# The second attention's result turned by VectorE squares and a way through memory

## The chip, the cores and the metric

The kernel runs on one core of one Trainium2 chip. The metric is the device time of one execution in microseconds, the median of three runs. The engines are TensorE (matrix products and its own transposes), VectorE, ScalarE, GpSimd and SyncE (SP). SP only issues transfers here; they run on the core's 16 DMA engines.

## The reference

Two layers act on x, 8 images of 128 channels and 48 x 48 = 2304 positions, all in fp32. This is what is computed, cut to what matters:

```
# layer 0: causal attention over the 2304 positions, added to x
q, k, v = lrelu(W{q,k,v} @ [group_norm(x), position rows] + b)
x = x + (softmax(mask(q^T k / sqrt(128))) * mask) @ v
# layer 1, on tokens t (2304 x 128 per image)
t = x as tokens
n = layer_norm(t)
t = t + softmax(n n^T) n                  # full attention, no weights
u = layer_norm(t) @ W^T                   # then batch norm over all tokens
y_i = sigmoid(u_i + y_{i-1} @ V^T)        # a recurrence along the tokens
return t + y
```

## The kernel before

**Chunks and batches.** An image is a batch b. Its 2304 positions are six chunks j of 384 tokens (NQ = 6, QC = 384), a chunk is three blocks of 128 (QB = 3). For each batch the class Causal does the first attention and the class Full the second, and a stream of items (one item is one block of keys or values against one chunk of queries) runs through all batches without a break. The first three items of the next batch's causal attention lie between the last items of the full one, and the projections of the next batch run in the full attention's chunks 4 and 5. After the last batch comes the recurrence in three groups.

**The order of the instructions.** It is written out by hand. Stream keeps a modelled time, now, and lists of pending steps (Chain), each with a cost and a due time. Each pass of the main loop emits the score product of item n, then the value product of item n - 3 (LAG), and then up to two due steps. Every engine works through its own instructions in just that order, and each transfer of SP waits at the head of SP's queue until what it needs is there.

**The full attention.** The score matrix is symmetric, so a square of it is used twice. For chunk j and a later chunk n the direct item makes scores (L1168), exponentials on ScalarE (L1170) and the product with the values (L1182). VectorE then transposes the square in 32 x 32 blocks (L1131), three of these make a tile, SP stores the tile as e(j,n) (L1111), and four loads bring it back transposed as g(j,n) (L1102). Chunk n then takes its products for the keys of chunk j from g (L1178). "Pair (1,5)" below is g(1,5): the squares of keys of chunk 1, used by chunk 5. There are three buffers for g, so a load can be issued when the third product with the tile three places before is done. Chunks 4 and 5 take four and five such tiles.

**The end of a chunk.** Full.after closes chunk j. ScalarE copies the result from PSUM (L1193). A chain of steps follows: the row sums (sums, with a small product on TensorE, L1205), then residual, in which TensorE transposes the result's three blocks (transposed, L931, the rows of_t), VectorE scales them, adds them to the tokens (L1224), takes the moments and makes a 32 x 32 transpose for the way to memory (L1231). Then come the roots on GpSimd (rooted), a small transpose of them on VectorE (turn_root, L1242), the stores of roots and turned rows (spread, three transfers at L1248 and four at L1251), their loads in another layout (fetch, L1255 and L1257), a product with the weights (L1264), a scaling and statistics on VectorE (L1265, L1266) and a copy on ScalarE (stored, L1270). Once in a batch, after chunk 1, the rows kept for the output are stored (L1288, L1289). The last two chunks of the last batch take a shorter way without memory.

**Buffers.** chunk_tile hands out the chunk's tiles by tag. It remembers the holder of each buffer and the number of steps that the holder's chain must have done, and emits these first when they are still pending. The product results have two PSUM banks (ps_o), the scores four (ps_s), other small results two (ps_t).

Of the kernel before, what the change touches and what calls it, by code (L numbers as in the profile page):

```python
# [14 lines left out]
F32 = mybir.dt.float32  # L15
AF = mybir.ActivationFunctionType
ALU = mybir.AluOpType
# [587 lines left out]
def fast_path(ctx: ExitStack, tc: tile.TileContext, x, pe, w_ffn, out, x_tok, w_qkv, w_pos, v_t, gamma_beta, flag):  # L605
    nc = tc.nc
    B, C, H, W = x.shape
    N = H * W
    P = 128
# [52 lines left out]
    with ExitStack() as actx:  # L662
# [107 lines left out]
        for r in roots:  # L770
            nc.gpsimd.memset(r, 0.0)

        st = Stream()
        order = ExitStack()
        order.enter_context(tc.manual_schedule())
# [5 lines left out]
        def group_norm(b):  # L781
            xt = xbuf[b]
            c = {}

            def part1():
                gs = small2.tile([P, NQ, 6], F32, tag="gn_st", name=f"gn_st_{b}")
                for j in range(NQ):
                    nc.vector.bn_stats(gs[:, j, :], xt[:, ts(j, QC)])
                mv = small.tile([P, 2], F32, tag="gn_mv", name=f"gn_mv_{b}")
                nc.vector.bn_aggr(mv, gs)  # L790
                c["mv"] = mv

            def part2():
                mv = c["mv"]
                tp = psum_t(f"gn_m_{b}")
                nc.tensor.matmul(tp[:, 0:1], grp, mv[:, 0:1], start=True, stop=True)
                mg = small.tile([P, 1], F32, tag="gn_mg", name=f"gn_mg_{b}")
                nc.vector.tensor_copy(mg, tp[:, 0:1])
                d = small.tile([P, 1], F32, tag="gn_d", name=f"gn_d_{b}")
                nc.vector.tensor_sub(d, mv[:, 0:1], mg)  # L800
                e = small.tile([P, 1], F32, tag="gn_e", name=f"gn_e_{b}")
                nc.vector.scalar_tensor_tensor(e, d, d, mv[:, 1:2], ALU.mult, ALU.add)
                c["mg"], c["e"] = mg, e

            def part3():
                tp = psum_t(f"gn_v_{b}")
                nc.tensor.matmul(tp[:, 0:1], grp, c["e"], start=True, stop=True)
                rs = small.tile([P, 1], F32, tag="gn_rs", name=f"gn_rs_{b}")
                rsqrt(small, rs, tp[:, 0:1], 1e-5, "gn")
                norm_of[b] = c["mg"], rs  # L810

            return [(part1, 0.0, [("DVE", 3.6)]), (part2, 0.15, [("DVE", 0.6)]), (part3, 0.15, [("DVE", 0.15), ("POOL", 0.9)])]


# [85 lines left out]

        def bounds(b):

            qk = small.tile([P, 2], F32, tag="qk", name=f"qk_{b}")
            nc.vector.tensor_reduce(qk, largest[b], AX.X, ALU.max)
            nc.vector.tensor_mul(bound[:, b : b + 1], qk[:, 0:1], qk[:, 1:2])

# [27 lines left out]
        def turned_back(src, name):  # L934

            tp = psum_t(name)
            out_ap = tp[:, :QC].rearrange("p (a g r) -> p g a r", a=R, g=QB)
            for g in range(QB):
                nc.tensor.transpose(out_ap[:, g], src[:, ts(g, P)], ident)
            return tp  # L940

        def by_block(tile_ap):

            return tile_ap.rearrange("p (g a r) -> p a g r", a=R, g=QB)
# [6 lines left out]
        class Causal:  # L951
# [37 lines left out]
            def product(self, j, m, o, p, ready, first, last):  # L989
                b, off = self.b, self.offset(j, m)  # L990
                nc.tensor.matmul(o[:, off:QC], vals[b][:, ts(m, P)], p[:, off:], start=first, stop=last)  # L991
                st.spend((QC - off) * US, ready)

                if first:
                    self.sums[j] = (p, None)
                    return
                if self.sums[j][1] is None:
                    self.whose[j] = {}
                    a = chunk_tile("acc", f"acc_{b}_{j}", self.whose[j], 1)
                    if off:  # L1000
                        nc.vector.tensor_copy(a[:, :off], self.sums[j][0][:, :off])
                    nc.vector.tensor_add(a[:, off:], self.sums[j][0][:, off:], p[:, off:])
                    self.sums[j] = (None, a)
                else:
                    a = self.sums[j][1]
                    nc.vector.tensor_add(a[:, off:], a[:, off:], p[:, off:])  # L1006
                st.then(ready, [("DVE", 0.15 + (QC - off) * 0.00105)])

            def after(self, j, o):
# [1 line left out]
                cols = ts(j, QC)  # L1011
                acc = self.sums.pop(j)[1]
                c = self.whose.pop(j)
                o_sb = chunk_tile("o", f"oc_{b}_{j}", c, 3)
                nc.scalar.copy(by_block(o_sb), o[:, :QC].rearrange("p (a g r) -> p a g r", a=R, g=QB))
                at = st.then(st.now, [("ACT", 0.5)])

                y = t1p.tile([P, QC], F32, tag="t1t", name=f"t1t_{b}_{j}")
                nc.sync.dma_start(y, x_tok[b, j])
# [17 lines left out]
                    c["ri"] = ri  # L1037

                def residual():
                    to = transposed(o_sb, f"oc_t_{b}_{j}")  # L1040
                    for g in range(QB):
                        nc.vector.scalar_tensor_tensor(
                            y[:, ts(g, P)], to[:, ts(g, P)], c["ri"][:, g : g + 1], y[:, ts(g, P)], ALU.mult, ALU.add
                        )
                    t1_tok[b, j] = y
                    c["mv"], c["ve"] = moments(y, f"c{b}_{j}", "l1")
# [12 lines left out]
                def back():  # L1059
                    tp = transposed(c["y"], f"tb_{b}_{j}")  # L1060
                    nc.scalar.copy(x_hat[b][1][:, cols], tp[:, :QC])

                c["chain"] = normed_chunks[b, j] = st.add([
                    (turn, 0.0, [("DVE", 1.05)]),
                    (sums, 0.15, [("DVE", 0.55)]),
                    (residual, 0.35, [("DVE", 2.6)]),
                    (rooted, 0.0, [("POOL", 0.9)]),
                    (normed, 0.0, [("DVE", 1.1)]),
                    (back, 0.35, [("ACT", 0.5)]),
# [2 lines left out]
        class Full:  # L1072
# [115 lines left out]
            def after(self, j, o):  # L1188
                b, rows, tsum = self.b, self.rows, self.tsum
                cols = ts(j, QC)  # L1190
                c = {}
                o_sb = chunk_tile("o", f"of_{b}_{j}", c, 2)
                nc.scalar.copy(o_sb, o[:, :QC])  # L1193
                at = st.then(st.now, [("ACT", 0.5)])
                last = b == B - 1 and j >= NQ - 2

                def sums():

                    dn = small.tile([P, QB], F32, tag="dn", name=f"dn_{b}_{j}")
                    nc.vector.tensor_reduce(dn, rows[:, QB * j : QB * (j + 1), : j + 1], AX.X, ALU.add)  # L1200
                    n = NQ - 1 - j
                    if n:
                        tp = psum_t(f"ts_{b}_{j}")
                        k = n * R * QB
                        nc.tensor.matmul(  # L1205
                            tp[:, :k], same.rearrange("p a c -> p (a c)"), tsum[j][:, :n, :].rearrange("p n k -> p (n k)"),
                            start=True, stop=True,
                        )
                        own = small2.tile([P, NQ - 1, R, QB], F32, tag="own", name=f"own_{b}_{j}")
                        nc.vector.tensor_mul(  # L1210
                            own[:, :n].rearrange("p n a g -> p (n a g)"), tp[:, :k], mine[:, :n].rearrange("p n a g -> p (n a g)")
                        )
                        more = small.tile([P, QB], F32, tag="more", name=f"more_{b}_{j}")
                        nc.vector.tensor_reduce(more, own[:, :n].rearrange("p n a g -> p g (n a)"), AX.X, ALU.add)
                        nc.vector.tensor_add(dn, dn, more)
                    ri = small.tile([P, QB], F32, tag="ri", name=f"ri_{b}_{j}")
                    nc.vector.reciprocal(ri, dn)
                    c["ri"] = ri

                def residual():  # L1220
                    tp = transposed(o_sb, f"of_t_{b}_{j}")
                    t2 = chunk_tile("t2", f"t2_{b}_{j}", c, 5 if last else 2, bufs=1)
                    for g in range(QB):
                        nc.vector.scalar_tensor_tensor(  # L1224
                            t2[:, ts(g, P)], tp[:, ts(g, P)], c["ri"][:, g : g + 1], t1_tok[b, j][:, ts(g, P)], ALU.mult, ALU.add
                        )
                    c["t2"] = t2
                    c["mv"], c["ve"] = moments(t2, f"f{b}_{j}", "l2")
                    if not last:
                        c["tt"] = chunk_tile("turn", f"tt_{b}_{j}", c, 5, bufs=1)  # L1230
                        nc.vector.transpose(  # L1231
                            c["tt"].rearrange("p (k g r) -> p g k r", k=R, g=QB), t2.rearrange("p (g k c) -> p g k c", g=QB, k=R)
                        )
# [17 lines left out]
                        nc.sync.dma_start(d[r], c["tt"][ts(r, SQ)].rearrange("c (k f) -> c k f", k=R))  # L1251

                def fetch():
                    c["t2x"] = chunk_tile("t2x", f"t2x_{b}_{j}", c, 7, bufs=1)
                    nc.sync.dma_start(c["t2x"], t2_d[:, b, cols])  # L1255
                    c["scale"] = chunk_tile("scale", f"scale_{b}_{j}", c, 8, bufs=1)
                    nc.sync.dma_start(c["scale"], c["rs_d"][0].partition_broadcast(P))  # L1257

                def product():
# [56 lines left out]
                else:  # L1316
# [5 lines left out]
                        (stored, 0.0, [("ACT", 0.85)]),  # L1322
                    ]
                c["chain"] = self.before["chain"] = st.add([
                    (sums, 0.15, [("DVE", 0.8)]),
                    (residual, 0.35, [("DVE", 3.2)]),
                    (rooted, 0.0, [("POOL", 0.9)]),
                    *steps,
                ], max(at, st.free["DVE"]) + 0.2 - st.now)
# [236 lines left out]
```

## Time and profile before

| | |
|---|---|
| median of three runs | 1795.67 us (1794.95 to 1795.85) |
| the profiled execution | 1795.9 us |
| its span | 1793.8 us |
| TensorE busy | 1757.0 us, 98% |
| VectorE, ScalarE, GpSimd busy | 1298.0, 751.6 and 217.0 us |
| bytes moved | 240.35 MB, 134 GB/s in the mean |
| TensorE's transposes of the second attention's result (L931, of_t) | 144, in 48 groups of three |
| VectorE's transposes of squares (L1131) | 360 of 128x384, 550 ns each |
| ScalarE's copies of the result (L1193) | 48, 479 ns each |
| turned rows to memory (L1251) | 184 transfers of 48 KB |

The span is from the first to the last instruction of the profiled execution. Busy times are sums over the span; those of TensorE are modelled, since products are pipelined. Times in the timelines count from the start of the span. The granted clock of TensorE was 0.991 in the mean.

### The profile page before, as it was taken

The page shows a single profiled execution, that of the slowest core. Times are in us where ns is not written, and L with a number is a line of the kernel's source. Part 1 is how long each engine was busy: PE and PEld are TensorE (multiplying, and loading weights), DVE is VectorE, ACT ScalarE, POOL GpSimd, SP SyncE. Part 2 cuts the span into 40 slices and gives each one's busy share as a digit, 9 for nine tenths or more (in the row PEclk, how much of TensorE's full clock was granted, in tenths as well). Part 3 has the DMA queues.
Part 4 walks back from the last instruction along what each step waited for, and adds up shares of the span by engine and source line. Part 5 has one row for each costly group of instructions (what it writes and reads, how often), then busy time and mean ns, then how long its engine had stood idle before and what let it go on. Part 6 is the DMA issues. An engine that isn't in the chain of part 4 may idle for free.

```text
span 1793.8 us, 22009 instructions
## 1 busy us (share of the span) xinstructions
PE 1757.0 (98%) x6363; PEld 1106.4 (62%) x6363; DVE 1298.0 (72%) x3321; ACT 751.6 (42%) x1852; POOL 217.0 (12%) x305
## 2 busy tenths in 40 slices
PE   8999999999999999999999999999999999999995
PEld 5666566665666566665666656665666656665574
DVE  5768668766887668686687668876686866876477
ACT  2344434443345424444344433454234443444354
POOL 1100011000210002000110002100020001100016
PEclk8999999999999999999999999999999999999998
DMA  4205662257314583056622573145830566025857
GB/s 151 102 1 190 180 166 82 74 181 192 109 62 132 162 217 106 1 188 179 167 83 74 182 187 113 63 132 163 216 106 1 183 183 172 27 72 182 201 179 200
DMA packets 176774, 240.35 MB, mean 134 GB/s; under 512 B 66209, under 2 KB 146242, under 8 KB 176644
## 3 DMA queue, kind: packets, MB, share of 16 engines
q1 hardware_dynamic: 175692, 235.83, 44.7%
q0 software_dynamic: 720, 2.62, 1.0%
q8 instruction: 53, 0.87, 0.2%
q14 instruction: 77, 0.63, 0.1%
q10 hardware_dynamic: 232, 0.40, 0.1%
HBM read 142.37 MB, written 96.41 MB: 133 GB/s over the span
## 4 chain that ended last, share of the span: by engine, by line
PE 95%; DVE 2%; DMA 1%; SPq 1%; issue 1%; ACT 0%; POOL 0%; DVEq 0%; ACTq 0%; POOLq 0%
PE s L1168 18%; PE o L1182 18%; PE s L980 17%; PE o L991 16%; PE o L1178 12%; PE pj L871 4%; PE pj L874 2%; PE z L1483 2%; PE wx L1264 2%; PE oc_t L931 1%; PE tb L931 1%; PE of_t L931 1%; SPq L1102 1%; DVE r L1465 0%; PE pb L829 0%
## 5 line engine op out<-in xcount | busy, mean ns | idle before, releaser
L1170 ACT ACTIVATE p<-s,shift 128x384 f32<-128x384 f32 x504 | 293.1, 582 | 491.3 <-PE s L1168 482.4
L982 ACT ACTIVATE p<-s 128x384 f32<-128x384 f32 (+2 forms) x504 | 233.0, 463 | 426.2 <-PE s L980 389.1
L1168 PE MATMUL s<-xh 128*128 128x384 f32 x1008 | 410.3, 489 | 0.0
L1182 PE MATMUL o<-p,xhT 128*128 128x384 f32 x1008 | 403.9, 487 | 4.4 <-ACT p L1170 4.4
L980 PE MATMUL s<-q,k 128*128 128x384 f32 (+2 forms) x1008 | 381.4, 460 | 0.1
L991 PE MATMUL o<-p,vT 128*128 128x384 f32 (+2 forms) x1008 | 378.3, 457 | 0.0
L1178 PE MATMUL o<-g,xhT 128*128 128x384 f32 x720 | 281.5, 488 | 1.4 <-DMA g<-e 1.3
L1182 PEld LDWEIGHTS o<-p,xhT 128*128 128x128 f32 x1008 | 189.0, 190 | 132.3 <-ACT p L1170 8.7
L991 PEld LDWEIGHTS o<-p,vT 128*128 128x128 f32 x1008 | 189.0, 191 | 114.7 <-issue 0.6
L1168 PEld LDWEIGHTS s<-xh 128*128 128x128 f32 x1008 | 186.1, 190 | 115.0
L1006 DVE TENSOR_TENSOR acc<-acc,p 128x384 f32<-128x384 f32 (+2 forms) x408 | 211.1, 517 | 48.9 <-ACT p L982 18.0
L980 PEld LDWEIGHTS s<-q,k 128*128 128x128 f32 x1008 | 180.9, 191 | 90.8 <-issue 0.9
L1131 DVE STREAM_TRANSPOSE t<-p 128x384 f32<-128x384 f32 x360 | 187.3, 550 | 37.6 <-ACT p L1170 36.2
L1178 PEld LDWEIGHTS o<-g,xhT 128*128 128x128 f32 x720 | 133.0, 190 | 84.1 <-issue 2.7
L1139 DVE TENSOR_REDUCE tsum<-t 128x12 f32<-128x1152 f32 x120 | 162.3, 1353 | 4.2
L876 DVE TENSOR_TENSOR z<-pj,pb 128x384 f32<-128x384 f32 x144 | 79.0, 548 | 105.2 <-PE pj L871 88.3
L985 POOL TENSOR_TENSOR p<-p,triu 128x128 f32<-128x128 f32 x144 | 83.4, 586 | 547.6 <-ACT p L982 417.2
L1237 POOL TENSOR_TENSOR roots<-ve_f,mhalf 128x3 f32<-128x3 f32 x48 | 40.8, 849 | 553.0 <-DVE ve_f L915 553.0
L1170 ACT ACTIVATION_READ_ACCUMULATOR p<-s,shift 128x1 f32 x504 | 98.0, 194 | 0.0
L871 PE MATMUL pj<-xn,wT 128*128 128x384 f32 x192 | 80.4, 504 | 1.4 <-DVE xn L864 1.4
L921 POOL TENSOR_TENSOR rs_c<-ve_c,mhalf 128x3 f32<-128x3 f32 x48 | 46.9, 977 | 245.7 <-DVE ve_c L915 245.7
L1224 DVE SCALAR_TENSOR_TENSOR t<-of_t,ri,t1t 128x128 f32<-128x128 f32 x144 | 41.5, 343 | 33.2 <-PE of_t L931 33.2
(262 smaller groups left out, 1492.2 us busy)
## 6 DMA issues: line engine op xcount, KB each, us to landing
e<-t SPq DMA_DIRECT2D x120, 576.0 KB
g<-e SPq DMA_DIRECT2D x480, 144.0 KB
pb<-posb_d SPq DMA_DIRECT2D x46, 576.0 KB
t1t<-in_x_tok_dram SPq DMA_DIRECT2D x48, 192.0 KB
t_d<-tt SPq DMA_DIRECT2D x184, 48.0 KB
t2x<-t_d SPq DMA_DIRECT2D x46, 192.0 KB
scale<-rs SPq DMA_DIRECT2D x46, 192.0 KB
x<-in_x_dram SPq DMA_DIRECT2D x14, 576.0 KB
```

What stands on the lines that cost most here:

```text
L871: nc.tensor.matmul(ps[:, :QC], wT[:, j, :], xn, start=True, stop=True)
L980: nc.tensor.matmul(s[:, off:QC], keys[b][:, ts(m, P)], queries[b, j][:, off:], start=True, stop=True)
L982: nc.scalar.activation(p[:, off:], s[:, off:QC], AF.Exp, scale=SCALE)
L985: nc.gpsimd.tensor_mul(p[:, off : off + P], p[:, off : off + P], triu)
L991: nc.tensor.matmul(o[:, off:QC], vals[b][:, ts(m, P)], p[:, off:], start=first, stop=last)
L1006: nc.vector.tensor_add(a[:, off:], a[:, off:], p[:, off:])
L1131: nc.vector.transpose(t[:, :, :, g, :].rearrange("p b j r -> p j b r"), p.rearrange("p (j b r) -> p j b r", j=QB, b=R))
L1139: nc.vector.tensor_reduce(self.tsum[j][:, n - j - 1, :], t.rearrange("p b j m r -> p (b j) (m r)"), AX.X, ALU.add)
L1168: nc.tensor.matmul(s[:, :QC], xh[:, ts(m, P)], xh[:, ts(j, QC)], start=True, stop=True)
L1170: nc.scalar.activation(p, s[:, :QC], AF.Exp, bias=shift, accum_out=self.rows[:, m, j : j + 1])
L1178: nc.tensor.matmul(out_ap, xhT[:, QB * i + g, :], p, start=first, stop=last)
L1182: nc.tensor.matmul(o[:, :QC], xhT[:, what[1], :], p, start=first, stop=last)
```

## The change

The result of a chunk of the full attention is no longer copied by ScalarE and transposed by TensorE. VectorE transposes it from PSUM in 32 x 32 blocks into an SBUF tile (turn_result). SP stores this tile to a tensor in memory, and four transfers load it back so that the blocks stand where a whole transpose would put them (token_major). These are two new steps ahead of sums, each with 5 us in the model. residual then reads the loaded tile (block_of) and emits no TensorE instruction. This is so for all chunks but the last three of the last batch, 45 of 48. The two flags are constants: CAUSAL_FAR is False, so the causal attention keeps its way, and FULL_FAR is True. Step counts given to chunk_tile rise by two where the chain is longer, and some small tiles move from a pool with three buffers to one with two.

```diff
+        def turn_result(o, name, holder, blocks_first):
+
+            ot = chunk_tile("o", f"ot_{name}", holder, 1)
+            dst, src = ot.rearrange("p (a g c) -> p a g c", a=R, g=QB), o[:, :QC]
+            if blocks_first:
+                dst, src = dst.rearrange("p a g c -> p g a c"), src.rearrange("p (g a r) -> p g a r", a=R, g=QB)
+            else:
+                src = src.rearrange("p (a g r) -> p a g r", a=R, g=QB)
+            nc.vector.transpose(dst, src)
+            return ot
+
+        def token_major(holder, ot, name, tag, steps):
+
+            d = dpool.tile([P, QC], F32, tag=f"o_{tag}", name=f"o_d_{name}")
+
+            def store():
+                nc.sync.dma_start(d, ot)
+
+            def load():
+                holder["o"] = to = chunk_tile(tag, f"to_{name}", holder, steps, bufs=1)
+                src = d.rearrange("(k r) (a f) -> a r k f", r=SQ, a=R)
+                for r in range(R):
+                    nc.sync.dma_start(to[ts(r, SQ)].rearrange("r (k f) -> r k f", k=R), src[r])
+
+            return [(store, 0.0, [("", 5.0)]), (load, 0.0, [("", 5.0)])]
+
+        def block_of(to, g):
+
+            return to.rearrange("p (k g c) -> p g k c", g=QB, c=SQ)[:, g]
...
-                o_sb = chunk_tile("o", f"of_{b}_{j}", c, 2)
-                nc.scalar.copy(o_sb, o[:, :QC])
-                at = st.then(st.now, [("ACT", 0.5)])
                 last = b == B - 1 and j >= NQ - 2
+                far = FULL_FAR and not (b == B - 1 and j >= NQ - 3)
+                if far:
+                    ot = turn_result(o, f"f_{b}_{j}", c, True)
+                    at = st.then(st.now, [("DVE", 0.57)])
+                    through = token_major(c, ot, f"f_{b}_{j}", "tof", 4)
+                else:
+                    o_sb = chunk_tile("o", f"of_{b}_{j}", c, 2)
+                    nc.scalar.copy(o_sb, o[:, :QC])
+                    at = st.then(st.now, [("ACT", 0.5)])
+                    through = []
+                F = len(through)
...
                 def residual():
-                    tp = transposed(o_sb, f"of_t_{b}_{j}")
-                    t2 = chunk_tile("t2", f"t2_{b}_{j}", c, 5 if last else 2, bufs=1)
+                    tp = None if far else transposed(o_sb, f"of_t_{b}_{j}")
+                    t2 = chunk_tile("t2", f"t2_{b}_{j}", c, 5 if last else 2 + F, bufs=1)
                     for g in range(QB):
+                        aps = t2[:, ts(g, P)], t1_tok[b, j][:, ts(g, P)]
+                        if far:
+                            aps = [i.rearrange("p (k c) -> p k c", k=R) for i in aps]
                         nc.vector.scalar_tensor_tensor(
-                            t2[:, ts(g, P)], tp[:, ts(g, P)], c["ri"][:, g : g + 1], t1_tok[b, j][:, ts(g, P)], ALU.mult, ALU.add
+                            aps[0], block_of(c["o"], g) if far else tp[:, ts(g, P)], c["ri"][:, g : g + 1], aps[1], ALU.mult, ALU.add
                         )
...
                 c["chain"] = self.before["chain"] = st.add([
+                    *through,
                     (sums, 0.15, [("DVE", 0.8)]),
-                    (residual, 0.35, [("DVE", 3.2)]),
+                    (residual, 0.0 if far else 0.35, [("DVE", 3.2)]),
                     (rooted, 0.0, [("POOL", 0.9)]),
                     *steps,
                 ], max(at, st.free["DVE"]) + 0.2 - st.now)
```

## The prediction

> **What bounds the kernel now.** I read the page's busy shares and slices, then the chain that ended last, then the groups, then TensorE and the SP queue in order of time.
>
> ```profile
> PE 1757.0 (98%) x6363; PEld 1106.4 (62%) x6363; DVE 1298.0 (72%) x3321; ACT 751.6 (42%) x1852; POOL 217.0 (12%) x305
> DMA  4205662257314583056622573145830566025857
> ...
> PE 95%; DVE 2%; DMA 1%; SPq 1%; issue 1%; ACT 0%; POOL 0%; DVEq 0%; ACTq 0%; POOLq 0%
> ```
>
> TensorE sets the end: 98% busy and 95% of the chain. A microsecond taken out of its queue is a microsecond off the span, and a new stall of TensorE is one on it. The transfers are busy only in waves, one for each batch.
>
> The removed triples, in the timeline of TensorE:
>
> ```profile
> 161.83 0.81 PE L1178 MATMUL o<-g,xhT 128*128 128x384 f32 x2
> 162.47 0.49 PE L931 MATMUL of_t<-ident,of 128*128 128x128 f32 x3
> 162.80 0.81 PE L1168 MATMUL s<-xh 128*128 128x384 f32 x2
> ```
>
> The start of the triple and the start of the next product lie 0.33 us apart (327 to 328 ns in 46 of the 48 triples). That is its price in the queue, not the 0.49 us of modelled busy time. A full product takes 0.645 us from start to start (162.80 to 163.45).
>
> Next, what already makes TensorE wait: few things, and two matter here.
>
> ```profile
> PE o L1182 <- ACT p L1170: 4.4, 7, 0.6
> PE o L1178 <- DMA g<-e: 1.3, 1, 1.3
> ```
>
> Last, the transfers of the stored squares where they are densest, chunks 4 and 5 of the second attention, in SP's timeline of batch 0:
>
> ```profile
> 211.91 0.41 SPq L1288 DMA_DIRECT2D out_dram<-t2c  x1
> 212.37 2.73 SPq L1289 DMA_DIRECT2D t2l_d<-t2c  x1
> 215.20 2.22 SPq L1102 DMA_DIRECT2D g<-e  x4
> ...
> 218.46 1.80 SPq L1102 DMA_DIRECT2D g<-e  x4
> 220.36 0.38 SPq L842 DMA_DIRECT2D pb<-posb_d  x1
> 220.83 0.38 SPq L1111 DMA_DIRECT2D e<-t  x1
> 221.91 6.72 SPq L1102 DMA_DIRECT2D g<-e  x8
> 229.46 1.56 SPq L1248 DMA_DIRECT2D rs<-roots_t  x3
> 231.06 1.87 SPq L1251 DMA_DIRECT2D t_d<-tt  x4
> ```
>
> The busy time by window over the same stretch (columns: TensorE, weight loads, VectorE, ScalarE, GpSimd, granted clock, DMA share, GB/s):
>
> ```profile
> 220.00:232.00 12.00, 12.00 (x45) 7.45 (x44) 8.13 (x23) 3.57 (x9) 0.85 (x1) 1.00 1.02 263
> ```
>
> SP is issuing almost without a pause and the transfer engines are full (1.02). The reader is to see that the second resource near its limit is SP's queue with the transfers behind it, in these 35 us of every batch. Taking the trace's packets in the order of the issues, the load for pair (1,5) can be issued when its buffer is free, at 226.1; it is issued from 226.3 to 228.7, lands at 232.1 and is used at 234.5. The one load that TensorE did wait for landed 1.3 us before the product started, so 1.3 us of each such distance is no reserve: about 1 us is left.
>
> [...] The trace has VectorE's 128x384 transpose at 550 to 577 ns against 0.33 us of TensorE. [...] in the built order the first load of each chunk does wait for its store. [...] the packets here put the landing of loads 1.7 to 4.5 us after their last issue, so I use those.
>
> **The change, part by part.**
>
> Removed from TensorE: 45 triples (48 chunks less the last three) x 0.327 = 14.7 us, all on the chain.
>
> Removed from ScalarE: 45 copies x 0.479 = 21.6 us; ScalarE is 42% busy and this is off the path.
>
> Added to VectorE: 45 transposes from PSUM. There is no row for that source; the rows from SBUF say 0.55 to 0.58, and I take 0.57, 25.7 us (bounds: ScalarE's copy of the same tile from PSUM, 0.479, and three VectorE pieces of it from PSUM, 3 x 0.343 = 1.03). VectorE has the room: 72% busy, and it loses its 33.2 us of waits for of_t. The result's PSUM bank is freed by VectorE and no longer by ScalarE, but it is next written two chunks later, over 5 us, so a late VectorE costs nothing there. If that cover were gone, 0.5 us a chunk.
>
> A stall that goes. Once in each of the first seven batches VectorE stands before a residual, and what is behind it is late:
>
> ```profile
> 196.36 0.87 DVE L1224 SCALAR_TENSOR_TENSOR t<-of_t,ri,t1t 128x128 f32<-128x128 f32 x3 [1.04 <-PE of_t L931]
> 199.70 1.14 ACT L1270 COPY wx<-scale 128x384 f32<-128x384 f32 x1 [2.62 <-DVE scale L1265]
> 200.03 0.81 PE L1178 MATMUL o<-g,xhT 128*128 128x384 f32 x2
> 201.47 0.91 PE L1182 MATMUL o<-p,xhT 128*128 128x384 f32 x2 [0.63 <-ACT p L1170]
> ```
>
> ScalarE waits for the scaled product behind the residual, exponentials queue behind ScalarE's copy, and TensorE starts 0.8 us late, and its next product 0.1 more. In the new order that product stands before the residual with little ahead of it on VectorE, so I expect 7 x 0.9 = 6.3 us back (at worst 0).
>
> Added to SP's queue: a store and four loads for each chunk, about 0.38 + 4 x 0.43 = 2.1 us, 95 us in all. SP has pauses for that except in chunks 4 and 5. There the chain of each chunk is later by two steps, so the order changes too. From the third product on pair (0,4), which frees a buffer, SP now issues in this order up to the load of pair (1,5): roots 1.56, turned rows 1.87, g(3,4) 1.80, the new store of chunk 3 0.38, the kept rows 0.41 + 2.73, g(0,5) 1.80, positions 0.38, the four new loads of chunk 3 1.75, e(4,5) 0.38, g(1,5) 1.80; with 0.6 us between them, 15.5 us. The first must wait for VectorE's small transpose of the roots, which stands behind a projection's two operations (0.56 each): 1.0 us. So the last issue is at 16.5. In full-queue conditions it lands 4.3 us later (bounds 2.2 and 5.5; positions and e, 1.2 MB, are ahead of it), plus 1.3: ready at 22.1 (bounds 20.0 and 23.3). TensorE, counted along the new order, has 27 full products x 0.645, two narrow ones x 0.42 and one sum x 0.29 = 18.55 us from the same point to its first product with pair (1,5). It would stall 3.6 us (bounds 1.5 and 4.8). In the kernel before, the kept rows and the roots of chunk 2 lay ahead of g(2,4) and g(3,4), whose buffers are free 10.3 and 11.3 us before use; here the distance is 9.1. After this stall the queue is caught up: for (2,5) I get 1 to 2 us to spare. Seven batches: 25.2 us, nothing if the transfers keep up.
>
> The last batch has no projections on TensorE to hide it, but only chunks 0 to 2 change. The kept rows move between (3,4) and (0,5), ahead of the roots of chunk 3; the same sum gives a stall of 3.9 where it now has 1.2: +2.7.
>
> Other added waits: the residual on VectorE waits for its rows. Behind it stand projections' additions, which free score banks. In the order the rows are issued 9 or more products (5.8 us) ahead of it, so 0; if they come late, VectorE stands still and TensorE has about two free banks, 1.3 us, before it follows. The smaller pools hold values of one batch or of VectorE alone: 0.
>
> Sum: -14.7 - 6.3 + 25.2 + 2.7 = +6.9. The profiled execution took 1795.9 (span 1793.8 and 2.1 around it), 0.2 above the median of 1795.67; so 1795.7 + 6.9 = 1802.6.
>
> **Rivals.**
>
> A, the likeliest: the load of (1,5) is late as computed, 2.4 to 4.8 us in a batch. 1793 to 1812. For it: SP's full row and a share of 1.02 in just this stretch.
>
> B, the other side: the same distance is longer than counted, since the loads need not follow positions and e at full length: 0.3 to 1.8 us a batch, 1.0 in the middle. -21.0 + 7 + 1 = -13: 1782.7 (1778 to 1789). For it: of all g loads, TensorE waited for one, 1.3 us, though SP was up to 4.0 us behind in chunk 4. It decides at 2.6 us a batch, (21.0 - 2.7) / 7: below that the change pays. Against it: the reserve before was 1 us, and 5 us of work are put into the distance.
>
> C: the detour is hidden wholly: -21.0, 1774.7. Against it: it needs the sum above to be 3.6 us too long.
>
> D: the waits for rows hold VectorE too, or the stall behind ScalarE's copy stays: A plus 6 to 12 us, 1809 to 1815. Against it: the distances in the order.
>
> **How the numbers follow.** A 0.52, B 0.28, C 0.08, D 0.12. The predicted time is A's, 1802.6. Range 1779 to 1814: A, nearly all of B and most of D; C and the ends of B and D are left out. A alone: 1793 to 1812. A measurement of this kernel tells 0.2% (3.6 us) from nothing. Faster: B, C and 0.02 of A, 0.38. Within: 0.10 of A. Slower: 0.52.
>
> **What would show it.** The of_t rows of TensorE fall from 144 to 9, and its wait for ScalarE's exponentials (4.4 us) is gone. A wait of a product with g for its load stands once in each batch near the start of chunk 5, 2 to 5 us, about 28 us in total; everywhere else TensorE is gapless. SP shows store and loads between the kept rows and g(1,5). I'm wrong if the waits for g stay under 10 us in total, if VectorE waits for the new rows by tens of us, or if TensorE waits for a PSUM bank.

## The result and the profile after

The changed kernel takes 1822.54 us (median of four, 1815.46 to 1825.14), the kernel before in the same session 1795.51 us. The ratio is 1.0145 with an interval of 1.0116 to 1.0174: 27.0 us slower. The forecast was 1802.6, in a range of 1779 to 1814: the direction was right, the time lies 8.5 us outside. The profiled execution took 1821.5, span 1819.8, granted clock 0.983 (0.991 before). Against the profiled execution of before, 1795.9, it is 25.6 us.

The page's lines that answer to those shown of before (busy times, the DMA slices, the chain):

```profile
PE 1756.9 (97%) x6227; PEld 1100.5 (60%) x6228; DVE 1317.2 (72%) x3366; ACT 737.5 (41%) x1807; POOL 206.1 (11%) x305
...
DMA  4205762268404673067622584046740676026757
...
PE 91%; DMA 6%; DVE 1%; SPq 1%; issue 0%; POOL 0%; ACT 0%; DVEq 0%; POOLq 0%; ACTq 0%
```

TensorE has 136 instructions less and is busy for as long as before. 6% of the chain that ended last now runs through transfers, 1% before. (That isn't all waiting, since the chain follows a transfer back to its issue: TensorE's own waits for transfers are 30.9 us, 1.7% of the span.) The changed parts did what they should, as two groups show (busy us, mean ns, idle before):

```profile
L951 DVE STREAM_TRANSPOSE ot_f<-o 128x384 f32<-128x384 f32 x45 | 26.1, 579 | 22.5 <-PE o L1226 21.7
...
L932 PE MATMUL of_t<-ident,of 128*128 128x128 f32 x9 | 1.5, 279 | 0.6 <-ACT of L1244 0.6
```

What TensorE waited for longest in the kernel after (total, times, longest):

```profile
PE o L1222 <- DMA g<-e: 30.9, 10, 4.8
```

The wait for ScalarE's exponentials (4.4 us) is gone. The wait for the stored squares has come, once in each of the first seven batches at the first product with g(1,5) (3.4, 2.4, 4.8, 4.3, 3.9, 3.7 and 3.9 us), for 0.5 us once more in batch 0, and twice in the last batch, 1.1 and 3.0. Here it is in batch 4, in TensorE's timeline of the kernel after:

```profile
1078.57 0.81 PE L1222 MATMUL o<-g,xhT 128*128 128x384 f32 x2
1083.24 1.65 PE L1222 MATMUL o<-g,xhT 128*128 128x384 f32 x2 [3.86 <-DMA g<-e]
1084.68 1.49 PE L872 MATMUL pj<-xn,wT 128*128 128x384 f32 x2
1085.96 1.49 PE L1212 MATMUL s<-xh 128*128 128x384 f32 x2
1087.24 1.49 PE L1222 MATMUL o<-g,xhT 128*128 128x384 f32 x2
1088.52 1.23 PE L1319 MATMUL wx<-t2x,w1T 128*128 128x384 f32 x2
1089.59 0.81 PE L1222 MATMUL o<-g,xhT 128*128 128x384 f32 x2
```

The reader is to see two things. The stall of 3.86 us was forecast, 3.6. What follows was not: four products in a row start 1.28 us apart (1084.68 to 1085.96) where a full product takes 0.645. The trace's clock records give TensorE half its clock from 1082.5 for 6.83 us. There are seven such stretches, at seven stalls, 3.41 or 6.83 us long and 34.1 us together; the kernel before has none between its first 60 us and its last 20. TensorE still stood for 3.2 us of the 34.1, which the waits already count. The other 30.9 us at half clock cost it about 15.5 us.

That closes the account of the profiled executions: -14.7 (triples), -4.4 to -6.3 (exponentials), +29.6 (waits for g, 30.9 against 1.3), +15.5 (half clock) make +24.1 to +26.0, where 25.6 was measured. The four times also go with their clocks: 0.985 at 1815.5, 0.983 at 1821.5, 0.981 at 1823.6 and 1825.1. An account is not yet a cause, though: had the clock stayed up, would those 15.5 us have been won?

SP's queue in the same stretch of the kernel after:

```profile
1061.09 1.55 SPq L1303 DMA_DIRECT2D rs<-roots_t  x3
1062.69 1.86 SPq L1306 DMA_DIRECT2D t_d<-tt  x4
1064.65 1.80 SPq L1146 DMA_DIRECT2D g<-e  x4
1066.50 0.42 SPq L959 DMA_DIRECT2D o_d_f<-ot_f  x1
1067.03 0.40 SPq L1343 DMA_DIRECT2D out_dram<-t2c  x1
1067.47 2.56 SPq L1344 DMA_DIRECT2D t2l_d<-t2c  x1
1070.46 1.81 SPq L1146 DMA_DIRECT2D g<-e  x4
1072.37 0.38 SPq L843 DMA_DIRECT2D pb<-posb_d  x1
1072.79 1.85 SPq L965 DMA_DIRECT2D to_f<-o_d_f  x4
1074.74 0.38 SPq L1155 DMA_DIRECT2D e<-t  x1
1075.22 3.87 SPq L1146 DMA_DIRECT2D g<-e  x4
```

This is the order of the forecast, and nearly its sum: 18.0 us from the roots to the last issue of g(1,5), against 15.5. But the last row is the telling one: four issues that take 1.80 us elsewhere took 3.87. SP itself was held back there. Its third issue stood 1.70 us until the transfer of the positions, eight transfers before it on SP's queue, had landed: in the trace both carry semaphore 108, and SP's transfers take eight such numbers in turn (100 to 105, 107, 108). SP's waits of the whole run have this once in each of the first seven batches at g(1,5), 0.75 to 1.9 us, and once more (total, times, longest):

```profile
SPq L1146 <- DMA pb<-posb_d: 10.8, 8, 1.9
```

The positions were issued at 1072.4 and landed at 1078.3, with the transfer engines full all the while. The busy time by window (TensorE, weight loads, VectorE, ScalarE, GpSimd, granted clock, DMA share, GB/s) shows it:

```profile
1060.00:1064.00 4.00, 4.00 (x18) 2.68 (x17) 3.58 (x8) 2.09 (x4) 0.00 (x0) 1.00 0.08 17
1064.00:1070.00 6.00, 6.00 (x20) 3.48 (x20) 4.33 (x8) 2.09 (x5) 0.00 (x0) 1.00 0.90 195
1070.00:1083.00 13.00, 9.38 (x35) 5.58 (x33) 5.90 (x15) 1.34 (x4) 0.00 (x0) 0.98 0.96 246
1083.00:1094.00 11.00, 10.76 (x24) 6.15 (x25) 5.10 (x16) 2.09 (x4) 0.00 (x0) 0.71 0.95 226
```

For 4 us the transfer engines are nearly empty (0.08), while SP waits for the roots and issues them; from 1064 on they are full for 30 us (0.90 to 0.96). (No run tests what these 4 empty us cost.) Taking the trace's packets in the order of the issues and their bytes, and adding up the time of each transfer's packets over the 16 engines, batch 4 has this between g(3,4) and g(1,5), both included:

| transfer | before, us of all 16 engines | after |
|---|---|---|
| g(3,4), g(0,5), g(1,5) | 2.75, 2.37, 2.85 | 2.42, 2.47, 2.11 |
| positions of chunk 2, e(4,5) | 2.37, 1.45 | 2.18, 1.68 |
| store and loads of chunk 3's result (new) | | 0.86, 0.88 |
| kept rows: t2c, t2l (stood ahead of g(2,4)) | | 1.90, 0.43 |
| sum | 11.8 | 14.9 |

In the kernel after, most of these packets run from 1065.1 to 1080.6, 15.5 us with hardly a gap. The last of g(1,5) come later, mixed with those of the next transfers: its landing is complete at 1083.20, and TensorE starts at 1083.24. Two theories stand, then, with nearly the same number: SP's issue time (the forecast's) and the engines' time.

### The profile page after: what moved, and what is told of

It reads as the page before. It is cut to its first block, busy times and chain, and to the rows that moved or that the text cites. A ratio compares the mean times of both kernels' runs of the same rounds, so it can differ in the third digit from the quotient of the medians.

```text
span 1819.8 us, 22052 instructions
## 1 busy us (share of the span) xinstructions
PE 1756.9 (97%) x6227; PEld 1100.5 (60%) x6228; DVE 1317.2 (72%) x3366; ACT 737.5 (41%) x1807; POOL 206.1 (11%) x305
## 4 chain that ended last, share of the span: by engine, by line
PE 91%; DMA 6%; DVE 1%; SPq 1%; issue 0%; POOL 0%; ACT 0%; DVEq 0%; POOLq 0%; ACTq 0%
PE s L1212 18%; PE o L1226 17%; PE s L1011 16%; PE o L1022 16%; PE o L1222 11%; PE pj L872 3%; DMA g<-e 3%; DMA pb<-posb_d 2%; PE wx L1319 2%; PE z L1539 2%; PE pj L875 1%; PE tb L932 1%; PE oc_t L932 1%; SPq L1146 1%; DVE r L1521 0%; DMA x<-in_x_dram 0%
## 5 line engine op out<-in xcount | busy, mean ns | idle before, releaser
L1222 PE MATMUL o<-g,xhT 128*128 128x384 f32 x720 | 291.4, 499 | 31.0 <-DMA g<-e 30.9
L1212 PEld LDWEIGHTS s<-xh 128*128 128x128 f32 x1008 | 190.5, 192 | 125.3 <-issue 4.2
L1016 POOL TENSOR_TENSOR p<-p,triu 128x128 f32<-128x128 f32 x144 | 71.2, 496 | 688.6 <-ACT p L1013 687.5
L1084 DVE SCALAR_TENSOR_TENSOR t1t<-oc_t,ric,t1t 128x128 f32<-128x128 f32 x144 | 41.6, 344 | 44.2 <-PE oc_t L932 44.2
```

What stands on the lines that cost most here:

```text
L1212: nc.tensor.matmul(s[:, :QC], xh[:, ts(m, P)], xh[:, ts(j, QC)], start=True, stop=True)
L1222: nc.tensor.matmul(out_ap, xhT[:, QB * i + g, :], p, start=first, stop=last)
```

## The experiments

All times are medians beside the kernel before on the same chip (1794.6 to 1795.6), and the changed kernel's 1822.5 is the reference. In the expectations "chunk 2's chain" as the old place of the kept rows is a slip: it is chunk 1's, whose chain stands at the same place in the order.

**1. Is the half clock a loss of its own?** Work for TensorE in place of the stall:

```diff
                     i, g = what[1:]
+                    if (i, j, g) == (1, NQ - 1, 0) and self.b < B - 1:
+                        idle(psum_s(f"fill_{self.b}"), 16)
```

> The changed kernel, with 16 products of the identity (128 columns each, 0.22 us, 3.5 us together, nothing reads them) put into TensorE's queue just ahead of the first product with g(1,5) in batches 0 to 6. Theory, that the stall itself is what halves the granted clock: the load is as late as before, but TensorE is busy for 3.5 of the 2.4 to 4.8 us that it stood, so the six records at half clock in batches 1 to 6 (27.3 us together, 13.7 us lost) go; where the stall is shorter than the filling (2.4 us in batch 1) the filling costs 1.1. 1821.5 - 13.7 + 1.1 = 1809 (1806 to 1812), a clock of 0.990. Rival, that the clock falls of itself or for the load on memory: 1821 to 1823, six records at half clock still there.

1817.68 us. The six stretches at half clock are gone; in this kernel they came with the stalls. Of the 12 to 14 us that they seemed to cost (27.3 us at half clock), only about 5 came back: 4.9 by the medians, with intervals that overlap (1.0099 to 1.0138 against 1.0116 to 1.0174). TensorE's timeline in batch 4 shows where the rest is:

```profile
1074.22 3.73 PE L1394 MATMUL fill<-ident 128*128 128x128 f32 x32
1078.80 0.91 PE L1224 MATMUL o<-g,xhT 128*128 128x384 f32 x2 [0.85 <-DMA g<-e]
...
1084.40 0.88 PE L1224 MATMUL o<-g,xhT 128*128 128x384 f32 x2 [0.81 <-DMA g<-e]
...
1089.67 0.88 PE L1224 MATMUL o<-g,xhT 128*128 128x384 f32 x2 [1.81 <-DMA g<-e]
```

At full clock TensorE runs up to the next late loads and stands there, 0.81 and 1.81 us. Waits of 14.5, filling of 7 x 3.5 and 3.4 for half clock at the end make 42.4, against 30.9 + 15.5 = 46.4 in the changed kernel. So the expectation's theory was right on the clock and wrong on the time: the whole row of loads up to g(3,5) is late, and the slow clock mostly hid the lateness behind the first.

**2. What was displaced, not what was added.** The kept rows stored in chunk 5's chain, outside the dense stretch:

```diff
-                    if j == SG // SJ - 1:
+                    if j == (SG // SJ - 1 if b == B - 1 else NQ - 1):
```

> The changed kernel, with the store of the kept rows (t2c, two issues of 3.1 us on SP) moved from chunk 2's chain to chunk 5's, so that it falls into the next batch's first attention; the last batch keeps its place. Theory, that the load of (1,5) is late by SP's queue: 3.1 us less ahead of it, the stalls of 2.4 to 4.8 us (mean 3.8 over seven batches) fall to 0 to 1.7, mean 0.7[...]; left are the triples (-14.7), the exponentials' wait (-6.3), 5 us of stalls, the last batch's 3 and its half clock (3.4): 1795.5 - 21.0 + 5 + 3 + 3 - 1 = 1785 (1779 to 1789). Rival, that the loads land late because the transfer engines are full with the added small packets: the same, since these bytes move away too. Rival, that the added steps of the chains delay something else: 1810 or more.

1794.16 us, 28 us less: the ratio to the kernel before is 0.9994 (0.9984 to 1.0005). It missed its 1785 since waits for g of 13.1 us stayed, not 8, and the last batch kept its own loss (experiment 6). Then the new way for chunks 0 to 2 alone, with none of chunk 3's transfers in the stretch but the kept rows in it, and for chunks 3 to 5 alone, the other way round:

```diff
-                far = FULL_FAR and not (b == B - 1 and j >= NQ - 3)
+                far = FULL_FAR and j < NQ - 3
```

> The changed kernel, with the new way only for chunks 0 to 2 of each batch (24 of 48), the old one with triples for chunks 3 to 5. In the built order chunk 3's store and four loads are gone from between g(3,4) and g(1,5), the kept rows are still there. Theory: from the third product on (0,4), 1.0 + 13.2 of issues + 4.3 + 1.3 = 19.8 us against 18.55 of TensorE: stalls of 1.3 us (up to 1.7)[...]. -24 x 0.327 = -7.9, -6.3, +7 x 1.5, +0: 1795.5 - 3.7 = 1792 (1787 to 1796). Rival, that only chunk 3's own transfers are late: no stall, 1781. Rival, that the detour costs wherever it is: half of the loss, 1809.

```diff
+                far = FULL_FAR and j >= NQ - 3 and not (b == B - 1 and j >= NQ - 3)
```

> The changed kernel, with the new way only for chunks 3 to 5 of batches 0 to 6 (21 of 48). In the built order the kept rows and the roots of chunk 2 are again ahead of g(2,4) and g(3,4); the store and the loads of chunk 3 and the store of e(4,5) stand ahead of g(0,5). Theory, transfers: 1.65 us of packets are added ahead of g(0,5), which had 0.4 to spare: stalls of 1.3 us, in all 7 x 1.5 = 10; -21 x 0.327 = -6.9: 1799 (1792 to 1803), no half clock. Rival, that the stall needs the kept rows in the stretch and the detour itself is free: 1788 (1786 to 1790).

1825.94 and 1795.40 us. Waits for g were 24.0 us in the first, with five stretches of 3.41 us at half clock, and 5.2 us in the second, with none. So the new store and loads of chunk 3 are not enough for the loss, and it comes without them; most of it hangs on the kept rows in this stretch, whose code the change doesn't touch. Two more steps in the chain of chunk 1 put them there. (The second run isn't a gain either: its 21 triples are worth 6.9 us, of which waits for g took 3.9; the rest wasn't traced.) The first run was worse than all its forecasts: the roots and rows of chunk 3, one chain later, now stand ahead of g(3,5), and TensorE waited 5.1 us more for exponentials in the next batch's first attention. What is left over of its 30 us was not taken apart.

**3. SP's time or the engines'?** The loads issued by GpSimd:

```diff
-                    nc.sync.dma_start(to[ts(r, SQ)].rearrange("r (k f) -> r k f", k=R), src[r])
+                    nc.gpsimd.dma_start(to[ts(r, SQ)].rearrange("r (k f) -> r k f", k=R), src[r])
```

> The changed kernel, with the four loads of each turned result issued by GpSimd and no longer by SP; the same bytes go the same ways. Theory, SP's issue time: 1.9 us less ahead of g(1,5), stalls 0.5 to 2.9, mean 1.9, of which one or two still halve the clock: 1821.5 - 7 x 1.9 - 10 = 1798 (1791 to 1803). Rival, the transfer engines: stalls and half clock as they were, 1817 to 1824. Rival, that GpSimd's powers come late behind its issues: VectorE's wait for roots grows by tens of us, 1815 or more.

1829.68 us. SP's time for them is gone from the stretch. In batch 4 the last issue of g(1,5) ends 15.0 us after the first issue of the roots, 18.0 in the changed kernel. The product still starts 21.8 us after that first issue, where it was 22.2, and the wait of TensorE is as long as it was:

```profile
PE o L1222 <- DMA g<-e: 31.6, 15, 4.5
```

The transfer engines are as full with the second issuer: a share of 0.98 from 1070 to 1084, where the changed kernel has 0.96 from 1070 to 1083. Why it is even 7 us slower is settled in part: its trace has 41.0 us at half clock, 34.1 in the changed kernel, and a new wait of TensorE for GpSimd of 1.5 us. VectorE's seven largest waits are within 5 us of what they were, so its roots did not come later. Then the two halves of the kept rows' store, which were to load SP and the engines in opposite proportion. First t2l alone is moved (2.5 us of SP, 0.43 of the engines), then t2c alone (0.4 of SP, 1.9 of the engines):

```diff
                     if j == SG // SJ - 1:
                         nc.sync.dma_start(out[0, :, :LM, b, :], self.t2c[:, :LM])
+                    if j == (SG // SJ - 1 if b == B - 1 else NQ - 1):
                         nc.sync.dma_start(t2l_d[:, :, b, :], self.t2c[:, LM:])
```

> The changed kernel, with only the second half of the kept rows' store moved to chunk 5's chain: t2l, an issue of 2.5 us on SP, but 64 KB, 0.45 us of the transfer engines. The first half (t2c, 0.4 us of SP, 320 KB, 2.0 us of transfers) stays between the store of chunk 3 and g(0,5). Theory, SP's issue time alone: 2.6 us less ahead of g(0,5) and g(1,5) in each of seven batches and less half clock: 1822.5 - 18 - 4 = 1800. Rival, the transfers alone: 0.45 us a batch, 1819. Where both are nearly equal at that place (in the trace t2l's packets follow its issue by 0.3 us just when those of t2c end), each alone gives 0.5 us a batch, 1819 (1815 to 1822), though both together gave 28.

```diff
-                    if j == SG // SJ - 1:
+                    if j == (SG // SJ - 1 if b == B - 1 else NQ - 1):
                         nc.sync.dma_start(out[0, :, :LM, b, :], self.t2c[:, :LM])
+                    if j == SG // SJ - 1:
                         nc.sync.dma_start(t2l_d[:, :, b, :], self.t2c[:, LM:])
```

> The changed kernel, with only the first half of the kept rows' store moved: t2c, 0.4 us of SP, 320 KB in pieces of 138 bytes, 2.0 us of the transfer engines. The second half (t2l, 2.5 us of SP, 0.45 of transfers) stays. Theory, SP's issue time alone: 0.45 us a batch, 1819. Rival, the transfers alone: 2.0 us a batch and less half clock, 1822.5 - 14 - 3 = 1805. Where both are nearly equal: 0.5 us a batch, 1819 (1815 to 1822).

1813.88 and 1804.53 us: -8.6 and -18.0. TensorE's waits for g, first with t2l moved, then with t2c moved:

```profile
PE o L1222 <- DMA g<-e: 25.3, 11, 3.5
```

```profile
PE o L1222 <- DMA g<-e: 20.8, 15, 2.7
```

"Both nearly equal" fell: each alone helps, and together they make 26.6 of the 28.4 that moving both gave. But the proportion was not what the expectations took it for. The issue of t2l takes 2.4 to 2.8 us in the changed kernel, where it comes right behind t2c; with t2c moved away it takes 0.6 us or less in each of the first seven batches:

```profile
1060.88 0.56 SPq L1345 DMA_DIRECT2D t2l_d<-t2c  x1
```

So both runs take about 2.5 us out of SP's row. They differ in the engines' time, by 1.5 us in each of seven batches, 10 us, and in the result by 9.4. That speaks for the engines more strongly than the comparison that was planned. What SP's own time is worth isn't separated: with t2l moved, the load of g(0,5) in batch 4 waited 2.3 us for its buffer instead, and the gain of 8.6 us contains a shorter time at half clock (20.5 us, 34.1 in the changed kernel). t2c's packets are 320 KB in pieces of 128 bytes (not 138, as the expectation has it) and take 1.9 us; e(4,5), 576 KB in pieces of 4608, takes 1.7: a KB in the small pieces took about twice as long.

A third step takes a transfer out where SP is ahead anyway, the positions of chunk 2 (0.38 us of SP, 2.0 to 2.4 of the engines). The first try put x in their place. The kernel's general path then ran behind the fast one, most likely because the bound on the scores came out too high, 6707.39 us in all, and the run says nothing of the question:

> The changed kernel, without the load of the third chunk's positions in batches 1 to 7 (one issue of 0.38 us on SP, 576 KB, 1.9 to 2.2 us of all transfer engines by its packets); the projection adds a part of x in their place, so its sums are others. The load stands between g(0,5) and g(1,5). Theory, that the transfers behind SP set the end: the packets of g(1,5) end 2 us earlier, each stall falls from 3.8 to 1.8, and the loads behind it by as much: 1821.5 - 6 to 7 x 2.3 - 3 = 1803 (1799 to 1808), at most two records at half clock. Rival, SP's issue time: 0.44 us less in a batch, 1818 (1815 to 1822), the half clock as it was.

The second leaves the positions of chunk 1 in use:

```diff
+                if n == 2 and b > 0:
+                    pos[b, n] = kept_pb[0]
+                    return
                 pos[b, n] = pbp.tile([P, 3, QC], F32, tag="pb", name=f"pb_{b}_{n}")
                 nc.sync.dma_start(pos[b, n], posb_d[:, n])
+                if n == 1:
+                    kept_pb[:] = [pos[b, n]]
```

> The changed kernel, without the load of the third chunk's positions in batches 1 to 7; the projection of chunk 2 adds those of chunk 1, which still lie there, so its sums are others. One issue of 0.38 us on SP, 576 KB, 1.9 to 2.2 us of the transfer engines, between g(0,5) and g(1,5), where SP is ahead of them. Theory, that the transfers set the time from there on: 2 us a batch at (1,5) and at the loads behind it, and less half clock: 1822.5 - 14 - 3 = 1805 (1800 to 1810). Rival, SP's issue time: 0.44 us a batch, 1819 (1816 to 1822).

1802.83 us, -19.7, where the theory of the engines said 1805 and that of SP 1819. One reserve: this is the transfer for whose landing SP stood in the changed kernel, so that wait goes too.

**4. The gain by itself.** The kernel before without its triples:

```diff
-                    tp = transposed(o_sb, f"of_t_{b}_{j}")
+                    tp = o_sb if not (b == B - 1 and j >= NQ - 3) else transposed(o_sb, f"of_t_{b}_{j}")
```

> The kernel before, without the 45 triples of TensorE transposes and nothing in their place: the residual reads ScalarE's copy as it lies, so the second attention's result is added untransposed. What the removal is worth alone. By the prediction's sum: -45 x 0.327 = -14.7, and up to -6.3 where the wait of VectorE for the triple was what held ScalarE: 1781 (1774 to 1782). Theory, transfers: two of the six triples in a batch stand in the stretch where the loads have 0.3 us to spare, so 0.65 - 0.3 of them come back as stalls: 7 x 0.35 = 2.5, 1783 (1777 to 1786), and waits for g of 3 to 6 us in all, from 1.3.

1779.56 us, -16.0, with 3.0 us of waits for g (1.3 before) and no wait for exponentials. The triples (14.7) and that wait (4.4), less 1.7, make 17.4: the gain side of the forecast holds to within some 3 us.

**5. Moves that should have paid and didn't.** The new way for chunks 4 and 5 alone, whose transfers lie outside the stretch (`j >= NQ - 2` in the condition; the DMA share of the kernel before is 0.39 from 250 to 260 us and 0.13 from 260 to 280), and a version with more of the transfers later in the order: kept rows late, last batch as before, and

```diff
-            return [(store, 0.0, [("", 5.0)]), (load, 0.0, [("", 5.0)])]
+            return [(store, 0.0, [("", wait)]), (load, 0.0, [("", 5.0)])]
...
-                        (spread, 0.0, [("", 10.0)]),
+                        (spread, 0.0, [("", 22.0 if j == 2 and b < B - 1 else 10.0)]),
```

with a wait of 16 for chunk 3.

> The changed kernel, with the new way only for chunks 4 and 5 of batches 0 to 6 (14 of 48). In the built order all the loads up to g(3,5) stand as in the kernel before; the store of chunk 4 is ahead of g(4,5), which lands 5.4 us (its packets' end) before its use, and the rest falls into the next batch's first attention, where the transfer engines idle. Theory: -14 x 0.327 = -4.6, nothing added: 1790.6 (1789 to 1792.5), faster than both. Rival, that the detour costs wherever it is: 1795 to 1803.

> A version meant to beat both: the new way for batches 0 to 6, the last batch as before; kept rows stored in chunk 5's chain; in the order, the four loads of chunk 3 and the load of the rows and the scale of chunk 2 come behind g(3,5) and no longer ahead of g(1,5) and g(2,5). The stretch from g(3,4) to g(3,5) then holds one transfer that it did not hold before, the store of chunk 3 (0.8 us), and no longer holds turned rows of chunk 3 (0.95). Theory, transfers: the 13 us of waits for g of the kernel with kept rows late fall to 0 to 4; -42 x 0.327 = -13.7, -6.3: 1795.5 - 20 + 3 = 1779 (1776 to 1785). Rival, that the later chains hold VectorE or the banks in the first attention: 1790 or more.

1799.76 and 1803.12 us. Both have few waits for g, 2.0 and 5.7 us, and a new one in the next batch's first attention: its small product dn waits for VectorE, for a PSUM bank that t1t or scale still reads, or for its own input, parts. The waits of TensorE, first of chunks 4 and 5, then of the later order:

```profile
PE dn L1070 <- DVE t1t L1084: 7.3, 7, 1.0
```

```profile
PE dn L1070 <- DVE parts L1064: 6.9, 8, 1.2
PE dn L1070 <- DVE scale L1320: 6.5, 7, 0.9
```

A chain pushed out of the dense stretch lands in the next stage, where VectorE has its own rush (92 to 95% busy from 260 to 290 us in the kernel before). In these two it isn't shown that this wait is the whole difference.

**6. Is that all of it?** Four runs settle what was open: kept rows late and the positions of chunk 2 out, with the last batch as before (`far = FULL_FAR and b < B - 1`); the same with these positions loaded; that with the load of chunk 3's positions 10 us later in the order, behind g(4,5); and these two moves in the kernel before.

```diff
-                pos_loads[b, n] = st.add([(f, 0.0, [])], st.free["DVE"] - st.now)
+                pos_loads[b, n] = st.add([(f, 0.0, [])], st.free["DVE"] - st.now + (10.0 if b and n == 3 else 0.0))
```

> The changed kernel with the kept rows stored in chunk 5's chain, without the load of the third chunk's positions (the projection of chunk 2 adds those of chunk 1, so its sums are others), and with the last batch as in the kernel before. 4.5 us of the transfer engines' time are out of the stretch from g(3,4) to g(1,5), 2.5 and 2.0. Theory, that the transfers in that stretch are the whole loss: waits for g under 5 us in all; -42 x 0.327 = -13.7 and the exponentials' wait of 4 to 6: 1795 - 19 = 1776 (1774 to 1781). Rival, that the change has another cost, on VectorE or in the banks: 1785 or more.

> The changed kernel with the kept rows stored in chunk 5's chain, and the last batch as in the kernel before. Beside the run with the kept rows late and three chunks of the last batch changed (1794.2): there the last batch lost 4.8 us against the kernel before, by the times of its score products, with a stall of 3.0 and a half clock. Theory: that is given back: 1794.2 - 4.5 = 1789.7 (1788 to 1792). Rival, that the loss at the end is not the change's: 1794 to 1795.

> The kernel before with the moves of e16: kept rows stored in chunk 5's chain (batches 0 to 6), and the load of the fourth chunk's positions 10 us later in the order, behind g(4,5). Theory: it has 1.3 us of waits for g in all, so there is nothing to win: 1795 (1793 to 1797). Rival, that it gains as well: 1790 or less.

> A version meant to beat both: the changed kernel with the kept rows stored in chunk 5's chain, the last batch as before, and the load of the fourth chunk's positions (576 KB, 2.0 us of transfers) 10 us later in the order, so that it stands behind g(4,5) and no longer ahead of g(3,5). Theory, transfers: half of what is left of the waits (about 10 us in the first seven batches with the kept rows late) stands at g(3,5) and goes, those at g(1,5) stay: 1789.7 - 5 = 1785 (1782 to 1788). Rival, that the first stall only makes the second: 1789 to 1791.

1777.89, 1789.63, 1796.35 and 1784.63 us, each within 2 us of its theory. TensorE's waits for g in the first and the last:

```profile
PE o L1228 <- DMA g<-e: 2.7, 5, 0.7
```

```profile
PE o L1222 <- DMA g<-e: 6.3, 7, 1.4
```

With 4.3 to 4.7 us of the engines' time out of the stretch the change gives 17.3 us, where the triples (13.7 in seven batches) and the exponentials (4.4 to 6.3) promise 18 to 20: another cost of more than some 3 us is not left to find. The last batch's three chunks cost 4.5 us, net of their triples. The moves alone win nothing in the kernel before (ratio 1.0003, 0.9995 to 1.0012). And the last version, with the whole computation, beats both kernels: 1784.63 us, ratio 0.9940 (0.9927 to 0.9954).

## Why the prediction was right and wrong

- **Removed triples, -14.7: right.** Taken out alone they gave 16.0, with the exponentials' wait gone and 1.7 us of new waits for g; nine of_t rows are left, as said. VectorE's transpose was to take 0.57 us and takes 0.579.
- **The stall behind ScalarE's copy, -6.3: right in kind.** Its 4.4 us are gone, in the changed kernel and without the triples; the 6.3 were not seen.
- **Added to SP's queue, a stall at g(1,5), +25.2 and +2.7: the place and the size were right, the size in part by luck.** It said 28 us of waits in all; they are 30.9. In batch 4 the stall was 3.86 us, forecast 3.6, but the terms were off and cancelled: SP's row from the roots took 18.0 us (15.5 forecast), the way from the last issue to the product 4.15 (4.3 + 1.3; 4.0 to 4.15 in all seven batches), and TensorE's distance was 19.0 (18.55). Three steps within it failed, and the second and third made the result wrong:
  - *The resource.* The distance was summed from SP's issue times, 15.5 us, with the transfers as a fixed 4.3 at its end. The engines' packets for the same transfers fill 15.5 us as well, and SP is held back by them (3.87 us for 1.80). Giving four loads a chunk to another issuer gained nothing; of two moves that freed SP about equally, the one with 1.5 us more of the engines' time gained 9.4 us more; two moves of some 2 us of the engines' time gave 18 to 20 each. Whether SP's time has a share of its own stays open. The share of 1.02 that the prediction quoted was the sum to make.
  - *"After this stall the queue is caught up: for (2,5) I get 1 to 2 us to spare."* The engines stay full up to g(3,5) (0.95 from 1083 to 1094 in batch 4); when the first stall was filled, TensorE stood at the later loads, and moving one transfer from ahead of g(3,5) gave 5.0 us.
  - *A stall was charged with its own length.* All but the first brought 3.4 or 6.8 us of half clock behind them, 15.5 us of TensorE's time in the trace, for which the sum had no term. This, 1.7 us more of added waits (29.6 against 27.9) and 1.9 less from the exponentials make 19.1; 18.7 is the excess of the profiled execution over the forecast's +6.9. The first run shows that the second and third failure are in the main one loss seen twice: about 5 us come back when the clock stays up.
- **The last batch, +2.7: the stall was right, the sum too small.** Its two stalls are 4.1 us, 1.3 before; the 6.8 us of half clock behind them had no term. Given back in the version with the kept rows late, it was 4.5, net of its triples.
- **Rivals.** B and C needed the transfers to be hidden, and they were not. D did not happen: VectorE's rows idle 0.6 us for the loaded result, and no bank wait shows in the changed kernel. Bank waits did come as soon as the chains were pushed later (dn for t1t, 7.3 us, and for scale, 6.5).
- **The range** took its upper end from waits alone. With the 15.5 us of half clock added, A itself would have been at 1818.1.

## What to carry to other kernels

Before transfers are added near a late load, sum the engine time of all packets between the moment its buffer is free and its use, beside the issue time of the queue; here, with a DMA share of 0.90 to 0.96, the engines were the sum that counted. Read an issue time from a row of issues with care: it can hold the time of the transfer ahead (t2l, 2.4 to 2.8 us behind t2c, 0.6 without it). Look for what a longer chain of steps pushes into the dense stretch: here moving one old store, which two new steps had shifted into it, gave the whole loss back. Price a stall of TensorE with what the clock may add: of the eight of 2.4 to 4.8 us here, seven brought 3.4 or 6.8 us at half clock.

## What the runs showed of the hardware

The longest stall of TensorE for g in each batch, and the half clock beside it, in the trace of the kernel after (us):

| batch | stall | product starts | half clock from | for |
|---|---|---|---|---|
| 0 | 3.41 | 234.15 | none | |
| 1 | 2.37 | 443.99 | 444.2 | 3.41 |
| 2 | 4.79 | 657.49 | 655.9 | 6.83 |
| 3 | 4.30 | 871.07 | 870.9 | 3.41 |
| 4 | 3.86 | 1083.24 | 1082.5 | 6.83 |
| 5 | 3.72 | 1296.70 | 1297.6 | 3.41 |
| 6 | 3.85 | 1508.95 | 1509.2 | 3.41 |
| 7 | 2.95 | 1718.12 | 1717.4 | 6.83 |

Each stretch starts between 1.6 us before and 0.9 us after the product that stood. The length of the stall alone doesn't sort them: 3.41 us in batch 0 kept the clock, 2.37 us in batch 1 lost it, and the longest two had 6.83 and 3.41 us. Shorter waits for g kept it: 0.54 and 1.07 us in this trace (batches 0 and 7), 1.3 us in the kernel before, and 0.85, 0.81 and 1.81 us in batch 4 with the filling (followed to 1091.5). What else decides isn't shown.
